# The last inverse transform: one tile for the base, a tile for each bank of transposes, products in two banks

## The chip, the cores and the metric

The kernel runs on one core of a Trainium2 chip. The metric is the device time of one execution in microseconds, the median of the runs. The engines are named as in the profile: PE is TensorE (PEld its weight loads), DVE VectorE, ACT ScalarE, POOL GpSimd, SP SyncE, which issues most transfers.

## What is computed

The network has two layers on x of shape (2, 128, 64, 64). The first normalises groups of channels and applies rotary attention with four heads. The second takes the 4096 pixels of each image as tokens, adds full self-attention over them, and then adds a spectral unit: a causal convolution of the tokens with 16 filters, each followed by a 128 x 128 matrix.

```
Vf = rfft(phi, n); Uf = rfft(u, n)
U_plus = irfft(Vf * Uf, n)[:sl]                     # 16 filters
out = einsum('btkd,k,kde->bte', U_plus, s, Mpp)     # and the same with alternating signs
out = out + sum_i einsum('btd,de->bte', shift(u, i), Mu[i])
...
return sum(stack(outs) * weights)                   # one of four branches weighs 1
```

The change touches only the very last step: the inverse transform of the spectral unit's output for one half of the second image, and its addition to what the other terms have already given, the base.

## The kernel before

After both attention parts, the kernel convolves in the frequency domain. For each of two images `b` and two halves `ro`, eight chunks `ch` of frequencies are processed, each for two streams `s`. `chunk` loads tables and tokens, `convolve` (L1186, L1195, L1196) multiplies them on TensorE into PSUM tiles `cv` and splits the result into a high part `xh` and a low part `xl`, and `mix` (L1218) multiplies these by the filters' matrices into the accumulator `acc` (its tile is named m). When both streams of a chunk are in, L1229 copies the accumulator to `oh`, 512 frequencies wide. The mixing of a chunk runs between the convolutions of the next one.

When a half is complete, `back` transforms it back. It does so in four parts `p4` of four blocks of 128 x 128. For each part `turned` loads the base (`had`, 256 KB) and transposes eight blocks of `oh` on TensorE (L1259) in two groups `c` of four, one PSUM bank each. VectorE copies the first group to SBUF and ScalarE the second (L1260), into `v`. `inverse` multiplies `v` by the inverse transform `gw` (L1268, eight products, each two instructions in the profile) into one bank `bk`, and VectorE adds the base and writes the result into `out` (L1270). For the first three halves this runs beside the next half's convolutions. The last one, `end`, has nothing beside it: the loop at the end of `layers` runs the last chunk's mixing and then `back` to its finish. After its fourth part, four stores of 512 KB, two from SyncE and two from ScalarE, write the image.

The program order of TensorE's instructions is kept as written (`ordered`). On the other engines, too, the instructions run in the order of the program; what starts when is set by the buffers. A pool gives each tag as many buffers as `bufs` says, and a new tile waits for all users of the buffer's former one. The PSUM pool `pc` holds one bank for `bk`, one for `acc`, and three buffers of two banks for `cv`. The SBUF pool `pf` holds two buffers `xh` of 32 KB per partition, used by the chunks in turn.

In the end, before the change, the transposes of part `p4 + 1` are issued ahead of the products of part `p4`. Both groups of a part lie in one tile `pair` of the tag `cv`, the two `v` take the two `xh` buffers by turns, and `had` has a single buffer.

Of the kernel before, what the change touches and what calls it, by code (L numbers as in the profile page):

```python
# [12 lines left out]
F32 = mybir.dt.float32  # L13
# [9 lines left out]
P = 128  # L23
B, C, HH, WW = 2, 128, 64, 64
# [14 lines left out]
BP = NI // 2  # L39
# [24 lines left out]
def conv_attn_hybrid(ctx: ExitStack, tc: tile.TileContext, io):  # L64
    nc = tc.nc
# [25 lines left out]
    def pool(stack, name, bufs=1, **kw):  # L91
        return stack.enter_context(tc.tile_pool(name=name, bufs=bufs, reuse_waits="tile", **kw))
# [641 lines left out]
    def layers(st, layer0):  # L734
# [344 lines left out]
        with ExitStack() as l1:  # L1079
# [3 lines left out]
            with ExitStack() as part:  # L1083
                p = pool(part, "l1_a")
# [25 lines left out]
            with ExitStack() as part:  # L1110
                p = pool(part, "l1_b", 2)
# [15 lines left out]
        pc = pool(st, "ff_psum", space=bass.MemoryType.PSUM)  # L1127
        pf = pool(st, "ff_x")
# [4 lines left out]
        def ordered(instruction):  # L1133
            return tc.keep_in_program_order(instruction)

        def one_bank(name):
            return pc.tile([P, 512], F32, tag="bk", name=name)
# [94 lines left out]
        def back(b, ro, oh, outs, p):  # L1232

            end = (b, ro) == (B - 1, 1)
            ohr = oh.rearrange("e (w p c) -> e c p w", c=2, p=BP)
            baser = base[b].rearrange("c (q r) j -> c r q j", r=2)
            if not end:
                for _ in range(WC + 1):
                    yield
            if ro == 0:  # L1240
                outs[b] = tokens[1].tile([P, L], F32, tag="t", name=f"out{b}")
            outr = outs[b].rearrange("p (j q r) -> p r q j", q=BP, r=2)

            def turned(p4):

                u = f"{b}_{ro}_{p4}"
                had = p.tile([P, 4, P], F32, tag="had", name=f"had{u}", bufs=1)
                nc.sync.dma_start(had, baser[:, ro, 4 * p4 : 4 * p4 + 4, :])

                v = (pf if end else p).tile(  # L1250
                    [P, 2, 4, C], F32, tag="xh" if end else "v", name=f"v{u}", bufs=2 if end else 1
                )
                if end:
                    pair = pc.tile([P, 2, 512], F32, tag="cv", name=f"vt{u}", bufs=3)
                for c in range(2):
                    pt = pair[:, c, :] if end else one_bank(f"vt{u}_{c}")
                    pt = pt.rearrange("p (q c) -> p q c", c=C)
                    for q in range(4):
                        ordered(nc.tensor.transpose(pt[:, q, :], ohr[:, c, BP - 1 - 4 * p4 - q, :], ident))  # L1259
                    (nc.scalar.copy if c else nc.vector.tensor_copy)(v[:, c, :, :], pt)  # L1260
                    yield had, v

            def inverse(p4, had, v):
                pt = one_bank(f"bk{b}_{ro}_{p4}").rearrange("p (q j) -> p q j", j=P)
                for q in range(4):
                    for c in range(2):
                        ordered(
                            nc.tensor.matmul(pt[:, q, :], v[:, c, q, :], gw[:, c, :], start=(c == 0), stop=(c == 1))  # L1268
                        )
                nc.vector.tensor_tensor(outr[:, ro, 4 * p4 : 4 * p4 + 4, :], pt, had, ALU.add)  # L1270

            ahead = list(turned(0)) if end else None
            for p4 in range(BP // 4):
                if end:
                    parts = ahead[-1]
                    ahead = list(turned(p4 + 1)) if p4 + 1 < BP // 4 else None
                else:
                    for parts in turned(p4):
                        yield
                inverse(p4, *parts)  # L1280
                yield
            if ro == 1:
                for i in range(4):
                    cols = bass.ts(i, L // 4)
                    (nc.scalar if i % 2 else nc.sync).dma_start(io["out"][b][:, cols], outs[b][:, cols])
# [6 lines left out]
        for b in range(B):  # L1292
            for ro in range(2):
                oh = (late_pool if ro else tokens[0]).tile(
                    [P, L], F32, tag="oh" if ro else "t", name=f"oh{b}_{ro}", bufs=1
                )
                for ch in range(NCH):
                    acc = pc.tile([P, 512], F32, tag="acc", name=f"m{b}_{ro}_{ch}")
                    for s in range(2):
                        u = f"{b}_{ro}_{ch}_{s}"  # L1300
                        halves = chunk(steps % 2, b, ro, ch, s)
                        xh = pf.tile([P, NK, WC * 4 * 2 * BP], F32R, tag="xh", name=f"xh{u}", bufs=2)
                        for _ in convolve(steps, u, halves, xh):
                            next(late, None)
                            next(beside, None)
                        late = mix(steps, ch, s, xh, acc, oh)
                        steps += 1
                for _ in beside:
                    pass
                if (b, ro) == (0, 0):  # L1310
                    right1.close()
                    late_pool = pool(right1, "out", 2, side="right")
                beside = back(b, ro, oh, outs, late_pool)
# [131 lines left out]
```

## Time and profile before

| what | us |
|---|---|
| median of three runs | 2932.92 (2932.57 to 2933.87) |
| the profiled execution | 2933.62 |
| its span | 2931.7 |
| TensorE busy in the span | 2856.0 (97%) |
| last mixing product ends, from the span's start | 2899.5 |
| last addition ends | 2921.15 |

The profile is one execution, recorded instruction by instruction. Its page gives shares of the span; further views give the instructions of a stretch in order of time, who waited for whom, and the chain of work that ended last, followed back from the last instruction. Times in these views count from the span's start. A busy TensorE is modelled at its ends, since matmuls overlap; the weight loads (PEld) show its pace. In the whole span the granted TensorE clock was 0.992 of full speed on average.

### The profile page before, as it was taken

How to read it: one execution, taken by the hardware profiler on the slowest of the kernel's cores; microseconds unless marked ns; L12 is line 12 of the kernel's file. 1: busy time of each engine (PE TensorE's matmuls, PEld its weight loads, DVE VectorE, ACT ScalarE, POOL GpSimd, SP SyncE). 2: the span in 40 equal slices, each digit the busy share in tenths (PEclk: the TensorE clock that was granted, in tenths of full speed). 3: DMA queues.
4: the chain of work that ended last, by engine and by line, in shares of the span. 5: the costliest groups of instructions: out<-in, count | busy, mean ns of one | idle time of the engine just before them, and what ended most of it. 6: DMA issues, size and time to landing. Idle time of an engine off the chain costs nothing. (4 is left out here: it accounts for less than half of the span.)

```text
span 2931.7 us, 40071 instructions
## 1 busy us (share of the span) xinstructions
PE 2856.0 (97%) x13872; PEld 1817.6 (62%) x13872; DVE 1689.6 (58%) x2916; ACT 1916.1 (65%) x2507; POOL 652.2 (22%) x1312
## 2 busy tenths in 40 slices
PE   5999999999999999999999999999999999999997
PEld 3555555555455578787777885666666666667665
DVE  5265562365243289777766776555555555555553
ACT  4999999999999956565555664444444444444442
POOL 3022120022000010000102003433444444444440
PEclk9999999999999999999999999999999999999999
DMA  4122120021000034100011002333333334333331
GB/s 136 33 67 73 54 63 13 5 78 48 6 33 35 4 94 124 49 1 1 26 40 38 8 26 76 90 93 95 85 89 82 82 83 111 81 85 83 82 84 43
DMA packets 166033, 175.91 MB, mean 60 GB/s; under 512 B 45264, under 2 KB 109536, under 8 KB 165824
## 3 DMA queue, kind: packets, MB, share of 16 engines
q1 hardware_dynamic: 122528, 137.05, 17.0%
q0 software_dynamic: 40304, 32.99, 5.5%
q10 hardware_dynamic: 2992, 3.22, 0.3%
q8 instruction: 115, 1.88, 0.3%
q14 instruction: 94, 0.77, 0.1%
HBM read 130.68 MB, written 25.49 MB: 53 GB/s over the span
## 5 line engine op out<-in xcount | busy, mean ns | idle before, releaser
L443 ACT ACTIVATE e<-s 128x1536 f16<-128x1536 f32 (+1 forms) x704 | 937.4, 1427 | 34.6 <-PE s L190 29.5
L1196 DVE TENSOR_TENSOR xl<-cv,xh 128x1024 fp32r<-128x1024 f32 x512 | 603.0, 1219 | 436.5 <-ACT xh L1195 349.1
L1195 ACT CAST xh<-cv 128x1024 fp32r<-128x1024 f32 x512 | 494.6, 1018 | 522.8 <-PE cv L1186 512.1
L1161 POOL DMA_DIRECT2D tokens_in<-rows x1024 | 489.1, 485 | 682.3 <-PE cv L1186 582.3
L190 PE MATMUL s<-qs,ks 128*128 128x512 f16 x2048 | 557.7, 379 | 11.9 <-ACT e L443 7.4
L190 PE MATMUL acc<-e,v 128*97 128x512 f16 x2048 | 557.3, 379 | 3.3 <-DVE accs L391 0.2
L1218 PE MATMUL m<-xh,loT 128*128 128x512 f32 x1024 | 409.5, 400 | 0.0
L1218 PE MATMUL m<-xh,hiT 128*128 128x512 f32 x1024 | 403.1, 394 | 0.0
L190 PEld LDWEIGHTS <-v 128*97 128x97 bf16 x2048 | 254.5, 124 | 214.4 <-issue 11.8
L190 PEld LDWEIGHTS <-ks 128*128 128x128 f16 x2048 | 200.5, 99 | 232.7 <-issue 47.2
L920 ACT ACTIVATE ey<-y,nshift 128x512 f32<-128x512 f32 x288 | 195.9, 689 | 201.5 <-PE y L911 179.3
L1186 PE MATMUL cv<-tables_in,tokens_in 32*128 32x512 f32 x2048 | 300.2, 646 | 1.8 <-DVE xl L1196 1.8
L1218 PE MATMUL m<-xl,hiT 128*128 128x512 f32 x1024 | 291.9, 417 | 1.2 <-DVE xl L1196 0.5
L1218 PEld LDWEIGHTS m<-xl,hiT 128*128 128x128 f32 x1024 | 178.7, 189 | 175.8 <-issue 104.7
L1218 PEld LDWEIGHTS m<-xh,loT 128*128 128x128 f32 x1024 | 192.5, 188 | 90.6 <-issue 47.8
L1218 PEld LDWEIGHTS m<-xh,hiT 128*128 128x128 f32 x1024 | 192.3, 188 | 42.2
L930 DVE TENSOR_TENSOR eT<-eT,eT 128x512 fp32r<-128x512 f32 x224 | 147.3, 683 | 112.9 <-ACT eT L929 112.0
L937 PE MATMUL oacc<-ep,hi 128*128 128x512 f32 x576 | 209.3, 412 | 1.2 <-DVE ep L969 1.2
L969 DVE TENSOR_TENSOR ep<-ey,ep 128x512 fp32r<-128x512 f32 x288 | 191.2, 683 | 7.8 <-ACT ep L968 1.6
L391 DVE COPY accs<-acc 97x512 f32<-97x512 f32 x64 | 44.2, 690 | 253.8 <-PE acc L190 253.8
L929 ACT ACTIVATE eT<-eT 128x512 fp32r<-128x512 f32 x224 | 133.1, 605 | 55.9 <-PE eT L927 55.7
L937 PE MATMUL oacc<-eT,hi 128*128 128x512 f32 x448 | 154.1, 405 | 2.1 <-DVE oT L975 1.2
(192 smaller groups left out, 3036.0 us busy)
## 6 DMA issues: line engine op xcount, KB each, us to landing
tables_in<-tables SPq DMA_DIRECT2D x1024, 64.0 KB, 3.3
tab<-in_rot SPq DMA_DIRECT2D x32, 512.0 KB, 4.1
tokens_in<-rows POOLq DMA_DIRECT2D x1024, 16.0 KB, 3.3
rows<-uh SPq DMA_DIRECT2D x64, 128.0 KB, 1.9
qs<-term POOLq DMA_DIRECT2D x112, 64.0 KB, 2.0
ks<-term POOLq DMA_DIRECT2D x96, 64.0 KB, 1.9
accs<-back SPq DMA_DIRECT2D x32, 128.0 KB, 2.3
lows<-stage SPq DMA_DIRECT2D x16, 256.0 KB, 2.0
```

The lines of the kernel that those rows point to most:

```text
L190: tc.keep_in_program_order(nc.tensor.matmul(*args, **kw))
L443: nc.scalar.activation(e[:, own, :], ps[:, own, :], AF.Exp, scale=SCORE_SCALE)
L920: nc.scalar.activation(e[:, 2 * h + q, :], ps[:, q, :], AF.Exp, bias=nshift, accum_out=den[:, t, i : i + 1])
L929: nc.scalar.activation(eT[0], pt, AF.Copy, accum_out=den[:, 4 * i + u, j : j + 1])
L930: nc.vector.tensor_tensor(eT[1], pt, eT[0], ALU.subtract)
L937: nc.tensor.matmul(acc, a[0][:, own], c, start=(start and t == 0 and n == 0), stop=(stop and t == len(es) - 1 and n == 2),)
L969: nc.vector.tensor_tensor(es[t][1], e[:, t, :], es[t][0], ALU.subtract)
L1161: nc.gpsimd.dma_start(ut[part, :, :], rows[b][ci, row : row + BP, w0 : w0 + WC // 2, :])
L1186: nc.tensor.matmul(pu[:, h, :], ut[grp, w % 2, :], tt[grp, w % 2, :], start=True, stop=True)
L1195: nc.scalar.copy(hi, pu.rearrange("d h (c k) -> d k h c", k=NK))
L1196: nc.vector.tensor_tensor(seconds[n % 2][:, :, w, 64 * g2 : 64 * g2 + 64].rearrange("d k (h c) -> d k h c", h=2), pu.rearrange("d h (c k) ...
L1218: nc.tensor.matmul(acc, m, x, start=(s == 0 and w == 0 and i == 0), stop=(s == 1 and w == WC - 1 and i == len(products) - 1),)
```

## The change

In the end alone, one tile `whole` in an `xh` buffer takes the base of all four parts and the turned parts as well, twelve blocks of 128 per part: four of base, eight of turned. Its four loads are issued at once. Each group of transposes gets a `cv` tile of its own (which uses one of the buffer's two banks). The products go by turns into `bk` and into the accumulator's bank. The order of transposes and products on TensorE is as it was; the loop is rewritten without yields. For the other halves nothing changes.

```diff
+            if end:
+                whole = pf.tile([P, BP // 4, 12, P], F32, tag="xh", name="whole", bufs=2)
+                for p4 in range(BP // 4):
+                    nc.sync.dma_start(whole[:, p4, :4], baser[:, ro, 4 * p4 : 4 * p4 + 4, :])
+
             def turned(p4):
 
                 u = f"{b}_{ro}_{p4}"
-                had = p.tile([P, 4, P], F32, tag="had", name=f"had{u}", bufs=1)
-                nc.sync.dma_start(had, baser[:, ro, 4 * p4 : 4 * p4 + 4, :])
-
-                v = (pf if end else p).tile(
-                    [P, 2, 4, C], F32, tag="xh" if end else "v", name=f"v{u}", bufs=2 if end else 1
-                )
                 if end:
-                    pair = pc.tile([P, 2, 512], F32, tag="cv", name=f"vt{u}", bufs=3)
+                    had, v = whole[:, p4, :4], whole[:, p4, 4:].rearrange("p (c q) x -> p c q x", c=2)
+                else:
+                    had = p.tile([P, 4, P], F32, tag="had", name=f"had{u}", bufs=1)
+                    nc.sync.dma_start(had, baser[:, ro, 4 * p4 : 4 * p4 + 4, :])
+                    v = p.tile([P, 2, 4, C], F32, tag="v", name=f"v{u}", bufs=1)
                 for c in range(2):
-                    pt = pair[:, c, :] if end else one_bank(f"vt{u}_{c}")
+                    pt = pc.tile([P, 512], F32, tag="cv", name=f"vt{u}_{c}", bufs=3) if end else one_bank(f"vt{u}_{c}")
                     pt = pt.rearrange("p (q c) -> p q c", c=C)
...
             def inverse(p4, had, v):
-                pt = one_bank(f"bk{b}_{ro}_{p4}").rearrange("p (q j) -> p q j", j=P)
+                tag = "acc" if end and p4 % 2 else "bk"
+                pt = pc.tile([P, 512], F32, tag=tag, name=f"bk{b}_{ro}_{p4}").rearrange("p (q j) -> p q j", j=P)
...
-            ahead = list(turned(0)) if end else None
-            for p4 in range(BP // 4):
-                if end:
-                    parts = ahead[-1]
-                    ahead = list(turned(p4 + 1)) if p4 + 1 < BP // 4 else None
-                else:
-                    for parts in turned(p4):
-                        yield
-                inverse(p4, *parts)
-                yield
+            if end:
+                parts = []
+                for p4 in range(BP // 4 + 1):
+                    if p4 < BP // 4:
+                        parts.append(list(turned(p4))[-1])
+                    if p4:
+                        inverse(p4 - 1, *parts[p4 - 1])
+            else:
+                for p4 in range(BP // 4):
+                    for parts in turned(p4):
+                        yield
+                    inverse(p4, *parts)
+                    yield
```

## The prediction

> **What bounds the kernel now.** I began with the page's first line and the chain of work that ended last, since the change touches only the last inverse transform, which runs after everything else.
>
> ```profile
> span 2931.7 us, 40071 instructions
> ```
>
> The profiled execution took 2933.62 us, so 1.92 us lie outside the span. Next I asked for the chain of waits in the last 34 us, in order of time (start, length, what):
>
> ```profile
> 2898.82 0.70 PE m L1218 x3
> ...
> 2899.55 0.59 ACT oh L1229
> 2900.14 0.04 issue
> 2900.19 0.72 PE vt L1259 x4
> ...
> 2900.93 0.70 DVE v L1260
> ...
> 2904.36 3.41 PE bk L1268 x16
> ...
> 2909.38 0.71 PE vt L1259 x4
> 2910.09 1.80 PE bk L1268 x16
> ...
> 2917.08 2.95 DMA had<-base
> ...
> 2920.13 1.02 DVE out L1270
> ```
>
> The last mixing product ends at 2899.52, ScalarE copies it to oh, and at 2900.19 the end begins alone on the chip. Its last addition ends at 2921.15: 20.96 us in which nothing else runs. Then four stores go out and the span ends at 2931.7, 10.55 us later. The chain passes from engine to engine: TensorE is never the bound for long. The waits of that stretch (who waits for whom: us in total, times, longest) say why:
>
> ```profile
> PEld vt L1259 <- DVE v L1260: 4.7, 4, 1.4
> PE vt L1259 <- DVE v L1260: 3.9, 4, 1.2
> DVE out L1270 <- DMA had<-base: 3.1, 1, 3.1
> PE bk L1268 <- DVE out L1270: 1.1, 1, 1.1
> ```
>
> Four times the second group of transposes waits until VectorE has copied the first group (0.79, 0.78, 1.19, 1.19 us of idle TensorE in the timeline), once the last product waits for the addition before it, and the last addition waits for its base. That base load can start only when the addition before has freed the one buffer `had` (2917.06), so its 2.95 us are bare from 2919.16, when the last product ends, to 2920.13: 0.97 us.
>
> One thing more is hidden in the chain: the first 16 product instructions took 3.41 us and the next 16 took 1.80. The table of stretches (busy us and counts of PE, PEld, DVE, ACT, POOL, then the granted TensorE clock) shows the cause:
>
> ```profile
> 2900.77:2904.18 3.41, 1.84 (x15) 1.53 (x14) 1.38 (x2) 0.59 (x1) 0.00 (x0) 1.00 0.00 0
> 2904.18:2907.59 3.41, 3.41 (x19) 3.41 (x18) 0.00 (x0) 0.59 (x1) 0.00 (x0) 0.50 0.02 5
> 2907.59:2911.00 3.41, 2.22 (x19) 2.03 (x18) 1.53 (x2) 0.59 (x1) 0.00 (x0) 1.00 0.21 63
> ```
>
> After a stretch in which weight loads filled only 1.53 of 3.41 us, the clock was halved for exactly 3.41 us. After stretches filled for 2.03 us and more it stayed whole.
>
> **What the Trainium skill says.** "TensorE: Matmul & The Clock Gate", section "What's actually happening": the clock is halved after a window of low activity, windows are 3413 ns and free-running, so where they fall differs from run to run. The trace agrees on the length (3.41 us) and on the cause (the sparse window before it). "PSUM — Partial Sum Buffer", section "PSUM bank collisions raise a hardware error": two engines must keep apart by bank, and different banks run clean. The two halves of `pair` are two banks of 512 f32 each, so the wait of the second group for VectorE's copy of the first comes from both sharing one tile, not from the memory. The trace before shows no case of it at this place, but in the main loop one engine reads `cv` while TensorE fills others.
>
> **The change, part by part.** First, what stays. The instructions of the changed program as built are the same on every engine up to the end, in the same order. In the end too: 32 transposes, 32 products (64 instructions), 4 copies on VectorE, 4 on ScalarE, 4 additions, 4 loads and 4 stores, in the same order on each queue. Only buffers, and so waits, differ.
>
> *One tile for base and turned parts.* The tile takes the `xh` slot of the last but one chunk. SyncE's first load there waits for the last reader of that slot, the mixing products that end in the timeline just before the next chunk's at 2888.10, so about 2887.6. Ahead of them on SyncE's queue are only table loads, done by then; behind them only the output stores. Four loads of 256 KB: one alone took 2.95 us, so between 2.95 + 3 x 0.36 (one issue) = 4.0 us together and 4 x 2.95 = 11.8 us one after the other. They land between 2891.6 and 2899.4; the first addition needs its base at 2904.1. What hides them are the mixing products, with 4.7 us to spare at the worst; without this cover they would cost the 0.97 us of today or more. The gain: 0.97 us.
>
> *A tile for each bank of transposes.* The second group no longer waits for the first copy. With three `cv` buffers the fourth group waits for the first copy, the fifth for the second, and so on in turn.
>
> *Products by turns in `bk` and `acc`.* The accumulator's bank is free from 2900.14, when ScalarE has copied it. A product then waits for the addition two before it.
>
> I laid the end out anew with the trace's own durations. TensorE issues by weight loads: 8 transposes took 0.97 us with 0.19 for one, (0.97 - 0.19)/7 = 0.111 each; 16 product instructions 1.87, (1.87 - 0.19)/15 = 0.112 each. So a group of 4 transposes issues in 0.45 us and its result is there 0.71 after its start; a product of 16 issues in 1.80 and ends after 1.95. VectorE copies in 0.69, ScalarE in 0.59, the addition takes 1.02 but lets a copy start 0.87 after its own start (2907.79 to 2908.66); a handover costs 0.02 to 0.04.
>
> Transposes 0a, 0b, 1a start at 2900.19, 2900.64, 2901.09. VectorE copies 0a from 2900.93 to 2901.62, so 1b starts at 2901.66 and not 2901.54: the only stall, 0.12 us. ScalarE has 0b by 2901.96, VectorE 1a by 2902.51, ScalarE 1b by 2902.99. Product 0 starts at 2902.11 and ends 2904.06; transposes 2a, 2b issue 2903.91 to 2904.81; product 1 starts 2904.81 in the other bank, its inputs ready since 2902.99, and ends 2906.76; transposes 3a, 3b issue to 2907.51. Addition 0 runs 2904.08 to 2905.10, copy 2a 2904.95 to 2905.62, addition 1 2906.78 to 2907.80, copy 3a 2907.65 to 2908.32. So product 2 (bank free at 2905.10, inputs at 2905.68) starts at once, 2907.51, and product 3 (bank free 2907.80, inputs 2908.40) at 2909.31, ending 2911.26. The last addition runs 2911.28 to 2912.30.
>
> The end is then bound by TensorE alone: 96 instructions x 0.112 = 10.75, one stall 0.12, 0.2 of drain and handover, 1.02 for the addition: 12.1 us against 20.96. The gain is 2921.15 - 2912.30 = 8.85 us. Against the old waits: transposes 3.95 less 0.12 kept, product 1.10, base 0.97, half clock 1.61 on the products and about 0.1 on the transposes behind them: 7.6. The other 1.2 are the drains of the five stalls, about 0.25 each (0.71 - 0.45 for a group of transposes), which a running TensorE covers.
>
> The half clock goes because no stretch of the new end is sparse: the longest gap is the old one before 2900.19 (0.67 us) plus 0.12. In the stretch 2897.36 to 2900.77, which held that gap, the clock stayed whole.
>
> The stores move up with the last addition; their 10.55 us stay. Nothing else is in their way, as the loads are done by then. The profiled execution becomes 2933.62 - 8.85 = 2924.77. It was 0.70 above the median of the runs; taking the same gain from 2932.92 gives **2924.1 us**, 0.30% faster.
>
> **Rivals.** *Half clock in the new end.* For: the windows run free, and the end follows a gap. Against: every window of it would be filled for well over 2.03 of 3.41 us. Price: one window at half clock loses 1.71 us, now all on the path: 2925.8. The same number results if the unprofiled runs of before had no half window to lose (8.85 - 1.71 = 7.14: 2925.8).
>
> *The waits stay.* If the copies into one tile were kept in order with each other or with the loads, or the two banks did not part, only the loads' gain would be left: 0.97, so 2932.0. Against: the built program has no wait of a copy on a load, and product 1 no longer waits on the addition. With the banks alone not parting, product 1 would wait for addition 0 (to 2905.14), product 2 for addition 1 and product 3 for addition 2, starting at 2911.20: 1.9 us lost, 2926.0.
>
> *Slower.* The new end is TensorE's alone, so its clock decides. At half clock throughout, 10.75 us become 21.5: the end takes 22.9 us, 1.9 more than now, 2934.8. The point is 8.85 us of loss, or 17.7 us of half clock, over five windows in a row; in before not two stood together while TensorE worked in the end.
>
> **How the numbers follow.** As forecast 0.78; half clock or nothing to lose, 0.14; a part or all of the waits stays 0.06; slower 0.02. Runs of before spread over 1.3 us. The range 2922.9 to 2926.6 holds the first two, with about 1 us below for the spread. Within 0.2% is within 5.9 us, about what measurement can tell from no change; the forecast and the half clock lie beyond it, with the smaller of the wait cases, so faster 0.93; same 0.05; slower 0.02.
>
> **What would show it.** Right: four loads issued near 2887.6 and landed before 2900; 16 transposes with one stall of about 0.1; all four products about 1.8 apart plus transposes; the last addition straight after the last product; the first transposes to the last addition's end near 12.1 us; clock whole. Wrong: an addition waiting for a load, a product for an addition, a half clock, or a stores' tail longer than 10.6 us.

## The result and the profile after

Over ten runs each, the median went from 2933.76 to 2925.11 us: 8.65 us less, a ratio of 0.9971 with a 95% interval of 0.9963 to 0.9980. The forecast was 2924.1 us, 8.85 less than the 2932.92 of the first three runs. Most of the miss of 1.0 us is the starting point: over ten runs the median before lies 0.84 higher than over three. The gain itself was 0.2 us less than forecast.

The first line of the page after:

```profile
span 2923.0 us, 40062 instructions
```

The span is 8.7 us shorter. The chain of waits after, in order of time (start, length, what):

```profile
2899.65 0.59 ACT oh L1229
2900.24 0.04 issue
2900.29 2.21 PE vt L1262 x16
2902.49 1.79 PE bk L1272 x16
2904.28 0.89 PE vt L1262 x8
2905.17 1.79 PE bk L1272 x16
2906.96 0.89 PE vt L1262 x8
2907.85 3.59 PE bk L1272 x32
2911.44 0.02 issue
2911.46 1.02 DVE out L1274
```

From the first transposes to the end of the last addition nothing but TensorE stands in the chain, until VectorE does the last addition. I call this stretch the end; it was 20.96 us (2900.19 to 2921.15) and is 12.19 (2900.29 to 2912.48). That is 8.77 less. The stores keep their length: from 2912.48 to 2923.0 it is 10.52 us, against 10.55. Some of the waits after (who waits for whom: us in total, times, longest):

```profile
ACT whole L1263 <- PE vt L1262: 5.9, 4, 2.1
DVE out L1274 <- PE bk L1272: 4.7, 4, 1.7
PEld vt L1262 <- ACT oh L1229: 1.1, 1, 1.1
```

TensorE's only wait left in the end is the one for `oh` at its start. The four waits of transposes for copies, the wait of a product for an addition and that of an addition for its load are gone. The clock in three stretches, with the columns of the table before:

```profile
2900.70:2904.12 3.42, 3.42 (x32) 3.34 (x30) 1.39 (x2) 1.17 (x2) 0.00 (x0) 1.00 0.02 5
2904.12:2907.53 3.41, 3.41 (x33) 3.41 (x32) 2.09 (x3) 0.59 (x1) 0.00 (x0) 1.00 0.00 0
2907.53:2910.94 3.41, 3.41 (x33) 3.41 (x33) 2.07 (x3) 0.59 (x1) 0.00 (x0) 1.00 0.02 5
```

Weight loads fill the stretches (3.34, 3.41 and 3.41 us), and the clock stays whole.

So far the forecast stands. But the prediction reached its number in two ways: by laying the end out anew, instruction by instruction ("the layout" below), and by adding up the old waits ("the sum of waits"). The two agree on the total, and need not agree on what each part of the change is worth.

### The profile page after: what moved, and what is told of

The parts are those of the page before. It is cut to its first block, busy times and chain, and to the rows that moved or that the text cites. A ratio compares the mean times of both kernels' runs of the same rounds, so it can differ in the third digit from the quotient of the medians.

```text
span 2923.0 us, 40062 instructions
## 1 busy us (share of the span) xinstructions
PE 2852.4 (98%) x13872; PEld 1815.1 (62%) x13872; DVE 1689.9 (58%) x2916; ACT 1916.1 (66%) x2507; POOL 653.8 (22%) x1312
```

## The experiments

The theory on trial says that the parts cover one another: take one wait away, and another that ran beside it comes to light. In the old end two chains ran abreast: copies and products in turn on one side, addition and load in turn on the other. The numbers of before say so. Here are the base loads of parts 1 to 3 on SyncE's queue, the first issued at 2908.83, and then the time from issue to landing of these three:

```profile
2908.83 8.61 SPq L1248 DMA_DIRECT2D had<-base  x3
```

```profile
DMA to landing us min/median/max: 2.9/3.0/3.0
```

So load 1 landed near 2911.8, and addition 1 began at 2911.92, just after its product. The profile names the product as releaser, but the load was only 0.1 us ahead of it. The rival says that the parts add up, as in the sum of old waits. To tell the two apart, each part was taken alone, and left out alone.

Up to the end TensorE's work is the same in all these kernels, and yet in the twelve profiled executions the end begins anywhere from 2897.54 to 2901.11 us. That is more than most of the effects looked for here, so the ends are compared, each from one profiled execution; the ratio of whole runs to before stands beside them, with its 95% interval.

### One tile for base and turned parts, alone

```diff
+                if end:
+                    pair = pc.tile([P, 2, 512], F32, tag="cv", name=f"vt{u}", bufs=3)
...
-                    pt = pc.tile([P, 512], F32, tag="cv", name=f"vt{u}_{c}", bufs=3) if end else one_bank(f"vt{u}_{c}")
+                    pt = pair[:, c, :] if end else one_bank(f"vt{u}_{c}")
...
-                tag = "acc" if end and p4 % 2 else "bk"
-                pt = pc.tile([P, 512], F32, tag=tag, name=f"bk{b}_{ro}_{p4}").rearrange("p (q j) -> p q j", j=P)
+                pt = one_bank(f"bk{b}_{ro}_{p4}").rearrange("p (q j) -> p q j", j=P)
```

(against the changed kernel: its second and third parts undone.)

> The end is measured from the first transposes' start to the last addition's end; it was 20.96 us before and 12.19 after. One tile for base and turned parts alone; both groups of a part share a tile and one bank takes all products, as before. Parts add up: only the bare 0.97 us of the last load go, end 20.0. Parts cover one another: the additions no longer wait for loads, but transposes still wait for the copies and products for the additions, laid out anew 17.9 at full clock, and 19.5 with the one half-clock stretch of before, which should stay since the first 4 us are as sparse as they were.

The end took 20.05 us (2899.31 to 2919.36), 0.91 less than before; the ratio of whole runs is 0.9997 (0.9988 to 1.0006). The sum of waits said 20.0 and was nearer than the layout with its 19.5. There was a half-clock stretch again:

```profile
2902.75 0.83 PE vt L1264 x4
2903.58 3.31 PE bk L1273 x16
```

The 16 product instructions took 3.31 us, not 1.80, and the four transposes before them 0.83, not 0.71. Without this the end would be about 18.4. The layout at full clock was 17.9, 0.5 too short; what it missed was not worked out.

### A tile for each bank of transposes, alone

```diff
-                if end:
-                    pair = pc.tile([P, 2, 512], F32, tag="cv", name=f"vt{u}", bufs=3)
...
-                    pt = pair[:, c, :] if end else one_bank(f"vt{u}_{c}")
+                    pt = pc.tile([P, 512], F32, tag="cv", name=f"vt{u}_{c}", bufs=3) if end else one_bank(f"vt{u}_{c}")
```

(against the kernel before.)

> A tile for each bank of transposes alone; base loads through one buffer and one bank of products as before. Parts add up: 3.83 us of waits, four drains of 0.25 and the half clock of 1.7 go, end 14.4. Parts cover one another: each base load still waits for the addition before it, so additions follow each other every 2.95 + 1.02 + 0.1 = 4.1 us, the first ending at 5.0 as the first product allows, end 17.3. No half clock in either.

The end took 17.40 us (2899.77 to 2917.17), ratio 0.9989 (0.9981 to 0.9998). If the parts cover one another 17.3 was expected; the sum of waits gives 14.4. The chain of waits of this run, its later part:

```profile
2909.11 2.91 DMA had<-base
2912.02 0.03 issue
2912.05 0.02 DVEq L1268
2912.07 0.04 issue
2912.11 1.03 DVE out L1268
2913.14 0.02 issue
2913.16 2.90 DMA had<-base
...
2916.15 1.02 DVE out L1268
```

Load, addition, load, addition: 4.04 us for each part. Once the transposes no longer wait, the additions wait for their loads.

### The change without its first part

(Own tiles and two banks together, put into the kernel before; base loads through the one buffer `had`, the turned parts in their old buffers.)

> The change without its first part: own tiles and two banks, but base loads through one buffer. Parts add up: the 0.97 us of the load come back, end 13.2. Parts cover one another: the chain of load and addition, 4.1 us for each part, decides and the banks are worth nothing: end 17.3, the same as with the tiles alone.

The end took 18.67 us (2900.42 to 2919.09), ratio 0.9990 (0.9983 to 0.9997). That is 6.5 us over the whole change, where the sum of waits allows 1.0. Its waits show three of the four additions waiting for their load:

```profile
DVE out L1269 <- DMA had<-base: 7.7, 3, 4.5
```

The third load was out of the usual here: 4.37 us, the two before it 2.93 and 2.92. With 2.92 the end would be 17.2, about as with the tiles alone, and 5.0 us over the whole change. Why it took longer no run tells. The median time of this kernel, 2930.07, is also near that of the tiles alone, 2930.43.

### The change without its second part

(Against the changed kernel: both groups of a part in one tile `pair`.)

> The change without its second part: one base tile and two banks, but both groups of a part in one tile. Parts add up: 3.83 + 1.0 + 1.7 come back on 12.2, end 18.7. Parts cover one another: laid out anew 16.6 at full clock, 18.3 with the half-clock stretch, so this one hardly tells the two apart; it tells whether the half clock goes with the sparse first 4 us: the clock is half for one window of 3.41 us if so, whole if not.

The end took 17.03 us (2901.11 to 2918.14), ratio 0.9991 (0.9983 to 1.0000). The layout said 16.6 at full clock and the clock stayed whole, although the gaps of the first two parts were there as before. That I had not expected; the clock has a section below. At full clock the sum of waits gives 12.2 + 3.83 + 1.0 = 17.0, nearer than the layout, which is 0.4 too short. So this run does not speak for either theory: leaving out the second part costs what the old waits of the transposes say.

### Products in two banks, alone

```diff
-                pt = one_bank(f"bk{b}_{ro}_{p4}").rearrange("p (q j) -> p q j", j=P)
+                tag = "acc" if end and p4 % 2 else "bk"
+                pt = pc.tile([P, 512], F32, tag=tag, name=f"bk{b}_{ro}_{p4}").rearrange("p (q j) -> p q j", j=P)
```

> Products by turns in two banks alone; shared tile and single base buffer as before. The end before was 20.96 us, 19.3 of it at full clock. Parts add up: the product's one wait of 1.10 and its drain of 0.25 go, 18.0 at full clock, 19.6 with a half-clock window. Parts cover one another: the last addition waits for its load whenever the product is done, so nothing is gained: 19.3, or 21.0 with a half-clock window.

The end took 19.33 us (2897.54 to 2916.87) at full clock, ratio 0.9999 (0.9991 to 1.0008). The sum of waits said 18.0. The second bank alone is worth nothing: the last product followed at once on the one before, and the last addition still waited for its load:

```profile
2911.77 1.06 DVE out L1271
2912.83 0.02 issue
2912.85 2.91 DMA had<-base
...
2915.86 1.01 DVE out L1271
```

### The change without its third part

(Against the changed kernel: all products in `bk`.)

> The change without its third part: all four products in one bank. Parts add up: 1.10 and 0.25 come back on 12.19, end 13.5. Parts cover one another: with the other two waits gone, products 1, 2 and 3 each wait for the addition before, as the prediction laid it out, 1.9 us: end 14.1. No half clock, or if one, 1.6 us more.

The end took 14.56 us (2900.23 to 2914.79), ratio 0.9980 (0.9972 to 0.9988). That is nearer to the layout's 14.1, which was 0.46 short, than to the 13.5 of the sum of waits. The chain of waits shows each product on its own behind an addition:

```profile
2904.27 1.03 DVE out L1273
2905.30 0.04 issue
2905.34 2.07 PE bk L1271 x16
2907.41 0.02 issue
2907.43 1.04 DVE out L1273
2908.47 0.04 issue
2908.51 2.07 PE bk L1271 x16
```

A product of 16 instructions that stands alone takes 2.07 us here until the addition can begin, one followed by others 1.79. A loop of product and addition is 3.17 us; three loops on the first addition's end make 9.5. The layout had 1.95 for a product and 3.03 for the loop.

### The gaps filled

```diff
+            if end:
+                idle = pc.tile([P, 8, P], F32, tag="cv", name="idle", bufs=3)
...
+                    if end and c == 0 and p4 < 2:
+                        for i in range(6):
+                            ordered(nc.tensor.transpose(idle[:, i, :], ohr[:, 0, i, :], ident))
```

(against the kernel before; `idle` takes one of the three `cv` buffers.)

> The kernel before with six transposes more in each of the first two gaps in which TensorE waits for a copy; their results are never read and they end before the copy does, so they lengthen no chain. Half clock from sparse windows: no half-clock window while TensorE works in the end, wherever the windows fall, and the end is 19.3 us. Half clock from something else: one window of 3.41 us at half clock as before, end 20.9.

The end took 19.38 us (2898.19 to 2917.57), all at full clock. The whole time, 2931.69 against 2932.89, cannot be told from no change (ratio 0.9997, 0.9988 to 1.0005). For what it says of the clock, see below.

### The last product split

In the changed kernel TensorE ends at 2911.44 and a whole addition follows. If this addition is cut up, most of it can run while TensorE works.

```diff
+            def last_inverse(p4, had, v):
+                for q0, q1, tag in ((0, 2, "acc"), (2, 3, "cv"), (3, 4, "cv")):
+                    pt = pc.tile([P, 512], F32, tag=tag, name=f"bk{b}_{ro}_{p4}_{q0}", bufs=3 if tag == "cv" else 1)
+                    pt = pt.rearrange("p (q j) -> p q j", j=P)
+                    for q in range(q0, q1):
...
+                    nc.vector.tensor_tensor(
+                        outr[:, ro, 4 * p4 + q0 : 4 * p4 + q1, :], pt[:, q0:q1, :], had[:, q0:q1, :], ALU.add
+                    )
```

> The change, with the last part's product in three PSUM banks, two blocks, one and one, and an addition after each, so that only a quarter of the last addition is left when TensorE ends. An addition of 512 columns takes 1.02 us; if a quarter takes a quarter and a little more, the end falls from 12.19 to about 11.5 us and the span with it; if most of its time is fixed, it stays near 12.2. In the times of whole runs 0.7 us is 0.02% and will hardly show; the profile must tell.

The end took 11.55 us (2900.60 to 2912.15), 0.64 less than the change. The median of whole runs was 2923.6, ratio to before 0.9970 (0.9957 to 0.9982). The groups of this run by shape (line, what, shapes and count, busy us, mean ns):

```profile
L1289 DVE TENSOR_TENSOR out<-bk,whole 128x512 f32<-128x512 f32 x3 | 3.1, 1043 | 3.9 <-PE bk L1287 3.9
L1277 DVE TENSOR_TENSOR out<-bk,whole 128x128 f32<-128x128 f32 x2 | 0.7, 370 | 0.1
L1277 DVE TENSOR_TENSOR out<-bk,whole 128x256 f32<-128x256 f32 x1 | 0.6, 601 | 0.0
```

A quarter of an addition takes 0.37 us, a half 0.60, a whole one 1.04: about 0.15 of each is fixed.

### The copy before the end split too

```diff
+                if n == 4 * B * NCH - 1:
+                    to, of = (x.rearrange("e (w p c) -> e w p c", c=2, p=BP) for x in (oh[:, bass.ts(ch, 512)], acc))
+                    for half in (slice(BP // 2, BP), slice(0, BP // 2)):
+                        nc.scalar.copy(to[:, :, half], of[:, :, half])
```

It ran beside the changed kernel itself.

> The changed kernel once more, beside the next one: end 12.2 us, time 0.9971 of before. From the end of the last mixing product to the end of the last addition it was 12.85 us.

> As with the split last product, and ScalarE copies the last accumulator to oh in two halves, the blocks that the first two parts need ahead. One copy took 0.59 us; if a half takes about 0.3 and the first transposes wait for their half alone, the time from the last mixing product to the last addition falls from 12.2 us with the split product alone to 11.9. If the transposes wait for both halves, or each copy has a fixed part near 0.2 us, it stays at 12.2 or rises to 12.4.

The changed kernel on its own repeated its end to the hundredth: 12.19 us (2901.08 to 2913.27), and 12.85 from the last mixing product's end at 2900.42; ratio 0.9970 (0.9958 to 0.9982). With both cuts it was 11.99 from the last mixing product (2897.58 to 2909.57), between the two expectations. The first half copy takes 0.38 us, where a half of 0.59 would be 0.30:

```profile
2897.61 0.38 ACT oh L1232
```

The median was 2922.91 against 2925.05 for the change, ratio to before 0.9965 (0.9952 to 0.9979). The ends say 0.86 us; the rest of the difference of 2.1 is within the spread of the runs, 2.0 and 3.3 us for the two kernels.

## Why the prediction was right, and where not

**The end bound by TensorE alone: right.** Laid out anew it was to take 12.1 us; it took 12.19. The one stall in the transposes is there, 0.16 us and not 0.12: 16 weight loads took 2.02 us, where 15 x 0.111 + 0.19 gives 1.86 without a stall.

**The loads hidden: right.** The four loads after:

```profile
L1247 SPq DMA_DIRECT2D whole<-base x4: 376/506/507, 2887.7 to 2889.2; - x4
...
DMA to landing us min/median/max: 3.2/3.9/4.4
```

The last was issued at 2889.2 and so was there by 2893.6, well before 2904.3, when the first addition began.

**The stores' tail unchanged: right,** 10.52 us.

**"The gain: 0.97 us" for the loads: wrong.** That is what the base tile gives alone (0.91), and not what it gives in the change. This table has the ends at full clock; where a half-clock stretch was recorded its cost is taken off, which is marked with a star. Each is one execution; only the last was measured twice, 12.19 both times:

| parts in | end, us |
|---|---|
| none | 19.38 (the gaps filled) |
| base tile | 18.4* |
| own tiles | 17.40 |
| two banks | 19.33 |
| own tiles, two banks | 17.2 (18.67 with the long load) |
| base tile, two banks | 17.03 |
| base tile, own tiles | 14.56 |
| all | 12.19 |

Alone the three gain about 1.0, 2.0 and 0.05: 3.0 us. Together they gain 7.2. Left out, they cost 5.0, 4.8 and 2.4. The intervals of the whole runs hold the gains of all rows and are too wide to test them further. Four runs tell the theories apart, and all four for covering: own tiles alone, two banks alone, and the change without its first or its third part. The base tile alone came nearer to the sum of waits, and the change without its second part fits the sum too.

The step that failed is to take each old wait (transposes 3.95, product 1.10, base 0.97) for what its part is worth. The 0.97 were only what stood out of a chain of load and addition, about 4.04 us for each part, that ran hidden beside the transposes' waits. The total came out right because all three parts were made at once: then TensorE's own work is what is left, and every old wait goes. The layout had foreseen which waits remain in the changed kernel; the worth of the parts was not to be read from the old waits.

The base tile is two things, early loads and a place of its own for every turned part. No run parts them; the additions wait for loads in the two runs where the tile is missing and the transposes are free, which speaks for the loads.

**"1.9 us lost" for one bank: undersized.** It was 2.37. The term mostly at fault is a product's time until its addition, 2.07 us and not 1.95, three times over.

**The half clock: gone as forecast, its place in the sum uncertain.** The changed end was at full clock in both profiled executions. (The prediction took comfort from the full clock of the stretch 2897.36 to 2900.77, which held the gap before the end. It is the next stretch that tells, and that was at full clock too.) But I took 1.7 us of gain from a stretch that was in the profiled run of before, and with the old gaps in place the stretch came in two executions (before, base tile alone) and not in two others (two banks alone, without the second part), where the windows fell otherwise. The prediction's rival had said that the runs without profile might have nothing to lose there, and gave 2925.8. Whether the median run before lost it cannot be read: the other runs carry only a mean clock of their whole span, rounded to 0.001, in which one stretch is 0.0006. The interval of the ratio, 5.9 to 10.9 us, holds both 7.2 and 8.8. So that the measured 8.65 lies so near to 8.85 is no proof of this term, and may be luck.

## What to carry to other kernels

Where several chains run abreast at about one pace, as here, the profile names the one that comes last, and a wait that it lists can be the excess of one chain over the next, not the worth of a change. Lay the stretch out anew with all its buffers, and don't read the worth of one part from its wait. What is left bare at the end of a kernel is worth cutting fine: the last addition and the copy ahead of it each gave some tenths of a microsecond with no more work for TensorE.

## What was not expected of the hardware

The windows of the TensorE clock lie differently from run to run, as the Trainium skill says in "TensorE: Matmul & The Clock Gate", section "What's actually happening". The traces agree: the window over the first two gaps begins 0.48 to 0.99 us after the end does, in five runs. What was new is how sparse a window must be for the clock to be halved after it. The page's table speaks of an idle window, which the prediction rendered as one of low activity; the runs show that after a window in which TensorE worked about half of the time the clock can be halved too. Below is the window over the first two gaps, and the one after it, in four runs beside the kernel before. The bounds are counted in steps of 3.413 us from the half-clock stretches that each trace records. The columns are as before: the figure after the first count is the weight loads' time, and the granted clock follows the last count. In order these are the runs with the base tile alone, with two banks alone, without the second part, and with the gaps filled; the window of the kernel before, 1.53 us filled, stands in the prediction.

```profile
2899.79:2903.21 3.42, 1.85 (x15) 1.47 (x14) 1.38 (x2) 0.59 (x1) 0.00 (x0) 1.00 0.00 0
2903.21:2906.62 3.41, 3.41 (x19) 3.41 (x18) 0.00 (x0) 0.59 (x1) 0.00 (x0) 0.50 0.02 5
```

```profile
2898.39:2901.81 3.42, 1.99 (x15) 1.80 (x16) 1.28 (x2) 0.63 (x2) 0.00 (x0) 1.00 0.00 0
2901.81:2905.22 3.41, 2.22 (x20) 2.03 (x20) 1.54 (x2) 0.54 (x1) 0.00 (x0) 1.00 0.02 5
```

```profile
2902.10:2905.51 3.41, 2.12 (x16) 1.94 (x17) 1.14 (x2) 0.80 (x2) 0.00 (x0) 1.00 0.00 0
2905.51:2908.92 3.41, 2.22 (x20) 2.03 (x19) 1.54 (x2) 0.37 (x1) 0.00 (x0) 1.00 0.02 5
```

```profile
2898.72:2902.13 3.41, 3.19 (x26) 2.80 (x25) 1.38 (x2) 0.58 (x1) 0.00 (x0) 1.00 0.00 0
2902.13:2905.54 3.41, 2.44 (x22) 2.24 (x21) 1.38 (x2) 0.59 (x1) 0.00 (x0) 1.00 0.02 5
```

After 1.53 and 1.47 us of weight loads in 3.41 the next window ran at half clock; after 1.80, 1.94 and 2.80 it did not. In the last run both gaps lay whole within the window, as in the kernel before and with the base tile alone (the window began 0.48 to 0.58 us into the end in these three, 0.85 and 0.99 in the other two). With the transposes put into the gaps the clock stayed whole: the same gaps left empty had cost 1.58 us (20.96 against 19.38). That is one execution, but in these five windows the fill and the clock go together.

From these alone one would put a limit between 1.53 and 1.80 us. But later in the run with two banks alone a window was filled for only 1.28 us, and the next one stayed whole:

```profile
2912.05:2915.46 3.41, 1.47 (x14) 1.28 (x12) 0.77 (x1) 0.00 (x0) 0.00 (x0) 1.00 0.29 82
2915.46:2918.87 3.41, 0.00 (x0) 0.00 (x0) 1.01 (x1) 0.00 (x0) 0.00 (x0) 1.00 0.36 138
```

So the time of the weight loads alone does not decide. The windows over the gaps hold mostly transposes and this one only products, so the kind of instruction may count; no run tests it, and it stays open.
